# A convolutional row LSTM: the even pixels' gate product moved to GpSimd, the input gate taken in two parts, a new written order

## Chip, cores, metric

The kernel runs on one core of one Trainium2 chip. The metric is the device time of one execution in microseconds; the median of the runs is quoted.

## What is computed

The input x has 8 images of 96 channels, 128 rows and 128 pixels, in float32. It is normalised in 32 groups of channels over each image (group norm). A masked 1x3 convolution of every normalised row gives the input's share of four gates; its mask lets a pixel see its left neighbour and, by thirds of the channels, itself. Then an LSTM runs down the rows: the state h of a row is convolved along the row with three taps (left, same, right), and

```
gates = conv3(h) + bias + row of the input's convolution
f, i, o = sigmoid(three of them); g = tanh(the fourth)
c = f * c + i * g
h = o * tanh(c)
out[row] = x[row] + h
```

Each row needs the row before it, 128 times in turn.

## The kernel before

**Half steps.** The batch is cut in two halves of four images (s = 0 and 1). A half step n is row n // 2 of half n % 2. The halves take turns, so that one half's elementwise work can lie beside the other's matmuls: n depends on n - 2. There are 256 half steps, R = 4 rows make a block, and blocks are loaded and stored whole.

**Even and odd pixels.** Pixels of a row are split into even and odd ones (64 of each), so a half step's operand is 256 columns for each parity. The three-tap convolution is computed by a short algorithm: from the state come `vs` (even plus odd, method `total`, L571), `vf` (odd minus even, `difference`, L583), and `vd` (two shifted differences, `shifted`, L587). Four products of these with prepared weights, 1, 2, 0 and 3 (`H_PRODUCTS`, L365), and one sum and one difference in between give both parities. The same is done for the input's convolution: `own_image` (L322) makes three operands of one row set out of x, `widen` (normalise into a work buffer `xw`, L297), then a sum (L315) and a pair of differences (L316). These feed the products P, Q and E. The other 32 channels of x, which all gates share, are normalised into the state's tile by `normalise_shared` (L340).

**Gates in banks.** The 384 gate channels are three tiles A, B, C of 128 rows, each in a PSUM bank of 512 columns (even 256, odd 256). Rows 0 to 95 of A, B and C are the gates f, i and o; rows 96 to 127 of each are a third of g. A half step is 33 products: 1, 2, 0, 3 for three tiles, each in two halves of 64 weight rows, and P, Q, E for three tiles with 64 rows. Two row groups of 64 rows work side by side; `Lanes` (L372) deals the products out in turn, and lets a product wait for the other row group where both add to one bank.

**A half step's chain.** For each tile: products 1, 2 (and P, Q); `copy` (L508, ScalarE, adds the bias, PSUM to SBUF); `even` and `odd` (L512 and L516, VectorE, in PSUM); products 0, 3, E on top; then ScalarE's `tanh` (L520) and `sigmoid` (L527, in place in PSUM). Then `forget` f * c (L532, VectorE), `gated` i * g (L537, VectorE), `cell` (L547, VectorE), `cell_tanh` (L552, ScalarE), `output` (L560, VectorE), and the next operands vf, vs (VectorE) and vd (GpSimd). `residual` (L607, GpSimd) adds h to x. The tile framework lets a product on a bank wait for the last vector operation on that bank, whichever half it wrote.

**The written order.** The compiler's scheduler is off (`manual_schedule`); each engine runs its instructions in the order in which they are written. The string `PERIOD` (L678) writes one half step n. A name is a part (`PARTS`, L685) with its tile: `1A` is product 1 of tile A (its first half at the first naming, the second at the next), `cpA` copy, `loA` even, `hiA` odd, `ta` tanh, `si` sigmoid, `fg` forget, `gt` gated, `ce` cell, `th` cell_tanh, `ou` output, `S`, `F`, `D` the next total, difference and shifted, `re` residual. A mark ' means half step n - 1, '' n - 2, + n + 1. A last letter a or b after some parts (`SPLIT`, L684) takes even or odd pixels alone. `W` calls `prepare(n - 1)`, which emits the preparation of the next block that `work` (L640) assigns to that half step: `own_image` of one image of the half, then the shared norm of one image. So GpSimd's order in a period is vd, residual, widen, sum, differences, shared norm.

**Start.** Ahead of the loop the statistics of all images are gathered from chunks of 1 MB, and the first rows are written out by hand (events, L815). `FIRST` (L629) gives the preparation of the first half steps, in which more has to be done than later.

Of the kernel before, what the change touches and what calls it, by code (L numbers as in the profile page):

```python
# [8 lines left out]
AF = mybir.ActivationFunctionType  # L9
# [12 lines left out]
def kernel(  # L22
# [103 lines left out]
    xs = pair([P, R, 3, BH, J], "xs")  # L126
# [4 lines left out]
    xw = [const.tile([P, R, W + 1], F32, tag=f"xw{i}", name=f"xw{i}") for i in range(2)]  # L131
# [29 lines left out]
    E = mybir.EngineType  # L161
# [147 lines left out]
            s * BH + j,  # L309
        )  # L310

    def combine(xw, n, total, differences):

        e, o = xw[:, 0:n, 0:J], xw[:, 0:n, J + 1 :]
        nc.gpsimd.tensor_add(total, e, o)  # L315
        nc.gpsimd.tensor_sub(  # L316
            differences,
            strided(xw[:, 0, :], 0, [(W + 1, n), (J, 2), (1, J)]),
            strided(xw[:, 0, :], J + 1, [(W + 1, n), (0, 2), (1, J)]),
        )  # L320

    def own_image(s, k, j):  # L322

        to = xs[s][k % 2]
        widen(nc.gpsimd, xw[0], 0, R, s, k, j, 0)
        combine(xw[0], R, to[:, :, 0, j, :], to[:, :, 1:3, j, :])

    def own_row(xw, s, r, lo=0, hi=BH):

        to = xs[s][0]  # L330
        combine(
            xw[:, lo:hi],
            hi - lo,
            to[:, r, 0, lo:hi],
            to[:, r, 1:3, lo:hi].rearrange("p t b j -> p b t j"),
        )
# [19 lines left out]
    HB = BH * J  # L356
    NT = NB * R
    last = NT * NH - 1
# [49 lines left out]
    class HalfStep:  # L408


        def __init__(self, n):
            self.n, (self.row, self.s) = n, divmod(n, NH)
            self.ps, self.m1, self.moving, self.done, self.gates, self.th = {}, {}, {}, set(), None, None
            self.started, self.images, self.halves, self.writer = set(), {}, {}, {}
            self.hx = hx[self.s][self.row // R % 2][:, self.row % R]
            self.xs = xs[self.s][self.row // R % 2][:, self.row % R]
            self.c = cs[self.s].rearrange("p t b j -> p (t b j)")
# [34 lines left out]
        def own(self, a, i):  # L452

            low = a == order["A"] or (a == order["C"] and (self.s == 0 or (self.n, i) == (1, 2)))
            rhs = self.xs[:, i].rearrange("p b j -> p (b j)")
            self.mm(a, i % 2, wo[i], rhs, slice(0, C2) if low else slice(C2, P))
# [63 lines left out]
            nc.scalar.activation(self.part(g, lo, hi, t), self.part(ps, lo, hi, t), AF.Tanh)  # L520


        def sigmoid(self, a):
            if self.row == 0 and a == 0:
                return
            gate = self.ps[a][0:C]
            nc.scalar.activation(gate, gate, AF.Sigmoid)  # L527

        def forget(self):
            f = self.ps[0][0:C]  # L530
# [3 lines left out]
        def gated(self, lo=0, hi=BH, t=None):  # L534
            to = self.g if self.row > 0 else self.c
            to, i, g = (self.part(ap, lo, hi, t) for ap in (to, self.ps[1][0:C], self.g))
            nc.vector.tensor_mul(to, i, g)  # L537


        def part(self, ap, lo, hi, t=None):  # L540
            ap = ap.rearrange("p (t b j) -> p t b j", t=2, b=BH)
            return ap[:, :, lo:hi] if t is None else ap[:, t, lo:hi]
# [44 lines left out]
        def shifted(self, lo=0, hi=BH):  # L587
            h = self.hx[:, 0, lo, :]
            diff = nc.gpsimd.tensor_sub(  # L589
                self.operand("vd", 2)[:, :, lo:hi],  # L590
                strided(h, 1, [(BH * JP - 1, 2), (JP, hi - lo), (1, J)]),
                strided(h, 0, [(BH * JP + 1, 2), (JP, hi - lo), (1, J)]),
            )
            if self.last.ins.engine != E.Pool:
                tc.add_manual_dep(
                    diff.ins,
                    self.last.ins.name,
                    mybir.DependencyInfo(
                        mybir.DependencyClass.Sync, mybir.DependencyReason.SCHED_ONLY
                    ),  # L600
                    reason="GpSimd starts when VectorE is done with both SBUF reads",
                )

        def residual(self):
            s, row = self.s, self.row
            xo = xt[s, row // R][0:C, :, row % R, :].rearrange("p b (j t) -> p t b j", t=2)
            (nc.gpsimd if 2 * row + s < last else nc.vector).tensor_add(xo, xo, self.h)  # L607

    def store(s, k, lo, hi):
        nc.sync.dma_start(  # L610
# [7 lines left out]
    SHARED = (((0, 0, R), (3, 0, 1)), ((1, 0, R),), ((2, 0, R),), ((3, 1, R),))  # L618
# [10 lines left out]
    FIRST = [  # L629
        own(0, 0),  # L630
        own(0, 1),
        own(0, 2) + shared(0, 1, 0, 1),
        own(0, 3) + [(load_rows, 0, 2)] + shared(0, 1, 2, 3),
        own(1, 0, 1),
        own(1, 2) + shared(1, 1, 0, 1),
        own(1, 3) + [(load_rows, 1, 2)] + shared(1, 1, 2, 3),
        [(own_image, 0, 2, 0), (own_image, 1, 2, 0)],
    ]

    def work(n):  # L640
        if n < len(FIRST):
            return FIRST[n]
        row, s = divmod(n, NH)
        k, r = divmod(row, R)
        parts = []
        if r == R - 1 and k + 2 < NB:
            parts.append((own_image, s, k + 2, 0))
        elif r < R - 1 and k + 1 < NB:
            parts.append((own_image, s, k + 1, r + 1))
        if k + 1 < NB:  # L650
            parts += shared(s, k + 1, *SHARED[r])
        if r == R - 2 and k + 2 < NB:
            parts.append((load_rows, s, k + 2))
        return parts

    worked = set()

    def prepare(n):
        if n not in worked:
            worked.add(n)  # L660
            for part, *args in work(n):
                part(*args)

    def finish(n):
        prepare(n)
# [19 lines left out]
    PARTS = {  # L685
# [57 lines left out]
    late = []  # L743
# [106 lines left out]
    n = m = 0  # L850
    for b in range(B):
# [7 lines left out]
        for k in range(QW // CH):  # L859
# [11 lines left out]
            if alone:  # L871
                i = list(shares).index(k)
# [25 lines left out]
    j = BH - 1  # L898
# [104 lines left out]
```

## Time and profile before

| What | us |
|---|---|
| median of 3 runs | 2024.15 (2023.83 to 2025.46) |
| the profiled execution's own time | 2027.04 |
| its span, first to last instruction | 2025.2 |
| granted TensorE clock | 0.997 |
| L508 copy, ScalarE, 128x256, mean of one | 0.474 |
| L527 sigmoid, ScalarE, 96x512 | 0.577 |
| L520 tanh, ScalarE, 32x512; 32x256 | 0.592; 0.369 |
| L552 cell_tanh, ScalarE, 96x256 | 0.411 |
| L512, L516 even, odd, VectorE, 128x256 | 0.425, 0.422 |
| L532 forget, VectorE, 96x512 | 0.696 |
| L537 gated, L547 cell, L560 output, VectorE, 96x256 | 0.412, 0.410, 0.412 |
| L573 vs, L585 vf, VectorE, 128x256 | 0.427, 0.429 |
| L589 vd, L607 residual, GpSimd | 1.041, 1.297 |
| L297 widen, L315 sum, L316 differences, GpSimd | 0.816, 0.641, 1.070 |
| L297 shared norm, GpSimd, 32x512 | 0.816 |

How it is read: the page gives busy time by engine, the chain of work that ended last, and the costliest groups of instructions; the timeline gives instructions in order of time, with the idle time before each and what ended it in square brackets. Equal instructions in a row are merged (x2, with the time from the first start to the last end). An operation on an engine may start before the one ahead of it has ended: two 128x256 operations on VectorE follow each other at about 0.33 us. Times in the timeline count from the span's start. In the half steps of the loop, from some 210 us on, one period looks like the next.

### The profile page before, as it was taken

Reading aid. Unit: us, or ns where it says so; the run is one execution under the profiler, and the core shown is the slowest. Engines: PE = TensorE matmul, PEld = TensorE weight load, DVE = VectorE, ACT = ScalarE, POOL = GpSimd, SP = SyncE. Lnnn points to the kernel's source line nnn. Section 1 sums busy time; section 2 is a strip of 40 time slices with the busy share of each in tenths; the row PEclk is TensorE's granted clock in tenths of the full one; section 3 lists DMA queues with packets and bytes.
Section 4 is the critical chain, followed back from the end, with each engine's and each line's share of the span. In section 5 each row is a group of like instructions: output and inputs, shape, how many; then the busy total and the mean of one; then the engine's idle time right before and its main releaser. Section 6 shows DMA issues by size and latency. Waiting matters only on the chain.

```text
span 2025.2 us, 44842 instructions
## 1 busy us (share of the span) xinstructions
PE 1923.3 (95%) x16936; PEld 1831.0 (90%) x16936; DVE 1529.1 (76%) x3996; ACT 1494.9 (74%) x3161; POOL 1473.1 (73%) x1712
## 2 busy tenths in 40 slices
PE   0289999999999999999999999999999999999998
PEld 0178999999999999999999999999999999999997
DVE  5767777777777777777777777777777777777776
ACT  3776777777777777777777777777777777777776
POOL 3348777777777777777777777777777777777752
PEclk9989999999999999999999999999999999999999
DMA  9994333444334334433433443343344333434411
GB/s 374 424 310 100 98 103 91 112 115 104 82 89 113 92 101 115 113 83 82 110 95 95 116 116 95 79 100 96 93 116 116 96 82 96 107 92 106 116 33 32
DMA packets 103382, 237.11 MB, mean 117 GB/s; under 512 B 5952, under 2 KB 8896, under 8 KB 97280
## 3 DMA queue, kind: packets, MB, share of 16 engines
q1 hardware_dynamic: 103168, 234.25, 42.0%
q8 instruction: 135, 2.21, 0.5%
q14 instruction: 79, 0.65, 0.1%
HBM read 183.90 MB, written 50.33 MB: 116 GB/s over the span
## 4 chain that ended last, share of the span: by engine, by line
PE 93%; DMA 4%; ACT 2%; DVE 1%; issue 0%; SPq 0%; POOL 0%; DVEq 0%; POOLq 0%
PE ps L442 92%; DMA piece<-in_x_dram 3%; DMA xs<-in_x_dram 1%; ACT piece L216 1%; PE ps L174 0%; ACT piece L217 0%; DVE bst L876 0%; ACT hx L295 0%; ACT piece L295 0%; DVE hx L560 0%; ACT xs L216 0%; ACT xs L217 0%; SPq L864 0%; PE pv L251 0%; DVE ps L516 0%
## 5 line engine op out<-in xcount | busy, mean ns | idle before, releaser
L442 PE MATMUL ps<-vd,wl 64*128 64x256 f32 (+1 forms) x6096 | 1390.9, 379 | 0.3
L442 PEld LDWEIGHTS ps<-vd,wl 64*128 64x128 f32 (+1 forms) x6096 | 1028.4, 186 | 45.7 <-issue 2.4
L442 PE MATMUL ps<-vs,wm 64*128 64x256 f32 (+1 forms) x3052 | 775.1, 380 | 4.9 <-POOL vs L573 4.4
L442 PE MATMUL ps<-vf,wm 64*128 64x256 f32 (+1 forms) x3052 | 766.3, 377 | 0.0
L527 ACT ACTIVATE ps<-ps 96x512 f32<-96x512 f32 x766 | 441.6, 577 | 356.2 <-PE ps L442 348.1
L442 PE MATMUL ps<-xs,wx 64*128 64x256 f32 x3080 | 637.8, 377 | 11.1 <-POOL xs L315 11.1
L589 POOL TENSOR_TENSOR vd<-hx 128x512 f32<-128x512 f32 x257 | 266.7, 1038 | 388.5 <-PE ps L442 384.8
L442 PEld LDWEIGHTS ps<-xs,wx 64*128 64x128 f32 x3080 | 494.0, 187 | 14.2 <-POOL xs L315 11.6
L520 ACT ACTIVATE g<-ps 32x256 f32<-32x256 f32 (+1 forms) x1021 | 468.6, 482 | 26.7 <-PE ps L442 6.3
L442 PEld LDWEIGHTS ps<-vf,wm 64*128 64x128 f32 (+1 forms) x3052 | 475.4, 187 | 11.0 <-PE ps L442 0.4
L442 PEld LDWEIGHTS ps<-vs,wm 64*128 64x128 f32 (+1 forms) x3052 | 459.6, 186 | 21.6 <-POOL vs L573 5.4
L512 DVE TENSOR_TENSOR ps<-m,ps 128x256 f32<-128x256 f32 x768 | 326.0, 425 | 192.5 <-ACT m L508 182.0
L442 PE MATMUL ps<-xs,wt 64*128 64x256 f32 x1530 | 453.2, 377 | 0.6 <-DVE ps L516 0.6
L508 ACT ACTIVATE m<-ps,wl 128x256 f32<-128x256 f32 x766 | 361.6, 474 | 90.9 <-PE ps L442 84.3
L532 DVE TENSOR_TENSOR ps<-ps,c 96x512 f32<-96x512 f32 x254 | 176.8, 696 | 232.9 <-PE ps L442 226.9
L607 POOL TENSOR_TENSOR x<-x,hx 96x512 f32<-96x512 f32 x255 | 330.8, 1297 | 6.7 <-DVE hx L560 6.7
L516 DVE TENSOR_TENSOR ps<-m,ps 128x256 f32<-128x256 f32 x768 | 300.8, 422 | 1.3 <-PE ps L442 1.2
L442 PEld LDWEIGHTS ps<-xs,wt 64*128 64x128 f32 x1530 | 280.0, 186 | 12.8 <-DVE ps L516 1.0
L316 POOL TENSOR_TENSOR xs<-xw 128x512 f32<-128x512 f32 (+1 forms) x254 | 270.9, 1067 | 0.0
L297 POOL TENSOR_SCALAR hx<-x,rstd,nmr 32x384 f32<-32x384 f32 (+2 forms) x312 | 225.8, 724 | 33.2 <-DMA x<-in_x_dram 1.1
L297 POOL TENSOR_SCALAR xw<-xr,rstd,nmr 128x512 f32<-128x512 f32 x252 | 205.6, 816 | 7.1 <-DVE nmr L289 6.5
L537 DVE TENSOR_TENSOR g<-ps,g 96x256 f32<-96x256 f32 x507 | 189.0, 413 | 3.8 <-ACT g L520 3.8
(91 smaller groups left out, 1223.1 us busy)
## 6 DMA issues: line engine op xcount, KB each, us to landing
xr<-in_x_dram SPq DMA_DIRECT2D x124, 512.0 KB, 6.4
x<-in_x_dram SPq DMA_DIRECT2D x63, 768.0 KB, 6.1
out_dram<-x SPq DMA_DIRECT2D x62, 768.0 KB, 4.6
xs<-in_x_dram SPq DMA_DIRECT2D x30, 1024.0 KB, 12.3
piece<-in_x_dram SPq DMA_DIRECT2D x16, 1024.0 KB, 12.3
x<-in_x_dram SPq DMA_DIRECT2D x62, 256.0 KB, 3.2
xs<-in_x_dram SPq DMA_DIRECT2D x4, 512.0 KB, 8.7
out_dram<-x SPq DMA_DIRECT2D x2, 576.0 KB, 3.7
```

Source lines behind the costliest of these rows:

```text
L297: return engine.tensor_scalar(dst, src, scale, shift, ALU.mult, ALU.add)
L316: nc.gpsimd.tensor_sub(differences, strided(xw[:, 0, :], 0, [(W + 1, n), (J, 2), (1, J)]), strided(xw[:, 0, :], J + 1, [(W + 1, n), (0, 2) ...
L442: made = nc.tensor.matmul(self.ps[a][:, bass.ts(half, HB)][:, cols], weights[rows, bass.ts(a, P)], rhs[rows, cols], start=new, stop=False, ...
L508: nc.scalar.activation(self.m1[a], m1, AF.Identity, bias=column)
L512: nc.vector.tensor_add(self.ps[a][:, 0:HB], self.m1[a], self.ps[a][:, HB:])
L516: nc.vector.tensor_sub(hi, self.m1[a], hi)
L520: nc.scalar.activation(self.part(g, lo, hi, t), self.part(ps, lo, hi, t), AF.Tanh)
L527: nc.scalar.activation(gate, gate, AF.Sigmoid)
L532: nc.vector.tensor_mul(f, f, self.c)
L537: nc.vector.tensor_mul(to, i, g)
L589: diff = nc.gpsimd.tensor_sub(self.operand("vd", 2)[:, :, lo:hi], strided(h, 1, [(BH * JP - 1, 2), (JP, hi - lo), (1, J)]), strided(h, 0, ...
L607: (nc.gpsimd if 2 * row + s < last else nc.vector).tensor_add(xo, xo, self.h)
```

## The change

- `gated` for even pixels goes to GpSimd. It reads the even half of the input gate from a new SBUF tile `i`, and g; the odd pixels' product stays on VectorE and reads PSUM.
- `sigmoid` of tile B is split: `siBa` writes the even half to that SBUF tile, `siBb` the odd half in place.
- `prepare` has three parts, called at `U`, `V` and `W`. In the steady loop U is empty, V emits the shared norm, W `own_image` and the loads. On GpSimd a period's order in the built program becomes vd, residual, shared norm, even gate product, widen, sum, differences.
- `PERIOD` is written anew. TensorE's order is 2A 2B 1A 1B 0C' 1A 3C' 2A 2B 0C' 1B 3C' 2C EC' 1C PB+ PC+ 1C 0A 2C 3A QC+ EA 3B QA+ EB QB+ 0B PA+ 3A 0B 0A 3B; ScalarE's siBa' taB' siA' siBb' cpA cpB taA' taCb' taCa' siC' cpC thb' tha'; VectorE's hiC' fg' loA hiA loB gtb' hiB ceb' cea' loC oub' oua' F' S'.
- `residual` waits for the total of the half step after it in the same half, where that was on VectorE (`hold`).
- The first half steps' preparation is spread differently: five shared norms of the second block go to ScalarE, and two images of half 1 are prepared in pieces with the second work buffer (`apart`, `LATER`).

Line numbers grow by up to 36: vf is L602 after, vs L590, vd L606, the sum L314, the differences L318, the gate product L552 or L554.

```diff
+    def add_pixels(xw, n, total):
+
+        nc.gpsimd.tensor_add(total, xw[:, 0:n, 0:J], xw[:, 0:n, J + 1 :])
+
+    def subtract_pixels(xw, n, differences):
+
         nc.gpsimd.tensor_sub(
             differences,
...
+    def combine(xw, n, total, differences):
+
+        add_pixels(xw, n, total)
+        subtract_pixels(xw, n, differences)
...
-        def sigmoid(self, a):
+        def sigmoid(self, a, lo=0, hi=BH, t=None):
             if self.row == 0 and a == 0:
                 return
-            gate = self.ps[a][0:C]
-            nc.scalar.activation(gate, gate, AF.Sigmoid)
+            gate = self.part(self.ps[a][0:C], lo, hi, t)
+            if t == 0:
+                self.even_input = self.tile("i", (C, HB))
+                to = self.even_input.rearrange("p (b j) -> p b j", b=BH)
+            else:
+                to = gate
+            nc.scalar.activation(to, gate, AF.Sigmoid)
...
-            nc.vector.tensor_mul(to, i, g)
+            if t == 0 and self.even_input is not None:
+                i = self.even_input.rearrange("p (b j) -> p b j", b=BH)
+                nc.gpsimd.tensor_mul(to, i, g)
+            else:
+                nc.vector.tensor_mul(to, i, g)
...
-            if self.last.ins.engine != E.Pool:
+            self.hold(diff)
+
+        def hold(self, made):
+            if self.last is not None and self.last.ins.engine != E.Pool:
                 tc.add_manual_dep(
-                    diff.ins,
+                    made.ins,
                     self.last.ins.name,
...
-            (nc.gpsimd if 2 * row + s < last else nc.vector).tensor_add(xo, xo, self.h)
+            made = (nc.gpsimd if 2 * row + s < last else nc.vector).tensor_add(xo, xo, self.h)
+            following = steps.get(self.n + NH)
+            if self.n < last and following is not None:
+                following.hold(made)
...
+    def on_scalar(s, k, *images):
+        return [(normalise_shared, nc.scalar, s, k, j, 0, R) for j in images]
+
+    def apart(s, k, j):
+        to = xs[s][k % 2]
+        return (
+            (widen, nc.gpsimd, xw[1], 0, R, s, k, j, 0),
+            (add_pixels, xw[1], R, to[:, :, 0, j, :]),
+            (subtract_pixels, xw[1], R, to[:, :, 1:3, j, :]),
+        )
+
+    spread = apart(1, 1, 0)
     FIRST = [
...
+        (on_scalar(0, 1, 0), [spread[0]], own(0, 3) + [(load_rows, 0, 2)]),
+        (on_scalar(0, 1, 1), list(spread[1:]), own(1, 1)),
+        (on_scalar(0, 1, 2) + on_scalar(1, 1, 2), shared(0, 1, 3), own(1, 2)),
+        (on_scalar(1, 1, 3), shared(1, 1, 0, 1), own(1, 3) + [(load_rows, 1, 2)]),
+        ([], [], [(own_image, 0, 2, 0)]),
     ]
+    LATER = dict(zip((11, 13, 15), apart(1, 2, 0)))
...
-        parts = []
-        if r == R - 1 and k + 2 < NB:
-            parts.append((own_image, s, k + 2, 0))
-        elif r < R - 1 and k + 1 < NB:
-            parts.append((own_image, s, k + 1, r + 1))
-        if k + 1 < NB:
-            parts += shared(s, k + 1, *SHARED[r])
+        early, late = shared(s, k + 1, *SHARED[r]) if k + 1 < NB else [], []
+        if n in LATER:
+            early.append(LATER[n])
+        ahead, image = (k + 2, 0) if r == R - 1 else (k + 1, r + 1)
+        if ahead < NB:
+            late.append((own_image, s, ahead, image))
         if r == R - 2 and k + 2 < NB:
-            parts.append((load_rows, s, k + 2))
-        return parts
+            late.append((load_rows, s, k + 2))
+        return [], early, late
...
-        "2A hiC' siA' D'' 1B 1A taA' 2B fg' 3C' 1A 0C' re'' taB' 2A 2B EC' 1B cpA 0C' 2C W loA cpB "
-        "3C' 1C siB' loB PB+ QA+ hiA taCb' 2C hiB taCa' 0A gtb' 1C siC' gta' EA 0B ceb' cpC 3A PA+ "
-        "cea' thb' PC+ 3B loC tha' QC+ oub' EB oua' QB+ 3A F' 3B 0A S' 0B"
+        "2A hiC' 2B 1A U siBa' 1B 0C' taB' D'' 1A 3C' siA' 2A 2B siBb' 0C' fg' 1B cpA re'' 3C' 2C "
+        "cpB V loA EC' 1C taA' PB+ hiA PC+ taCb' loB 1C 0A taCa' gtb' 2C 3A gta' W siC' hiB QC+ "
+        "EA ceb' cpC 3B cea' QA+ thb' loC EB tha' QB+ oub' 0B PA+ oua' 3A F' 0B 0A S' 3B"
...
-    SPLIT = ("taC", "gt", "ce", "th", "ou")
+    SPLIT = ("taC", "siB", "gt", "ce", "th", "ou")
...
-            if name == "W":
-                prepare(n - 1)
+            if name in "UVW":
+                prepare(n - 1, range("UVW".index(name) + 1))
                 continue
```

More of the change, by code (lines that the diff above doesn't have):

```diff
@@ L310, in widen @@
         )
-    def combine(xw, n, total, differences):
-        e, o = xw[:, 0:n, 0:J], xw[:, 0:n, J + 1 :]
-        nc.gpsimd.tensor_add(total, e, o)
+    def add_pixels(xw, n, total):
+        nc.gpsimd.tensor_add(total, xw[:, 0:n, 0:J], xw[:, 0:n, J + 1 :])
+    def subtract_pixels(xw, n, differences):
         nc.gpsimd.tensor_sub(
@@ L414, in __init__ @@
             self.started, self.images, self.halves, self.writer = set(), {}, {}, {}
+            self.even_input = self.last = None
             self.hx = hx[self.s][self.row // R % 2][:, self.row % R]
@@ L627, in shared @@
         ]
-    FIRST = [
[L630 to L637, printed above, removed]
+    def on_scalar(s, k, *images):
[8 more added lines that the diff above has]
+    spread = apart(1, 1, 0)
+    FIRST = [
+        ([], [], own(0, 0)),
+        ([], [], own(0, 1)),
+        ([], [], own(0, 2)),
+        (on_scalar(0, 1, 0), [spread[0]], own(0, 3) + [(load_rows, 0, 2)]),
[3 more added lines that the diff above has]
+        ([], [], [(own_image, 0, 2, 0)]),
     ]
+    LATER = dict(zip((11, 13, 15), apart(1, 2, 0)))
     def work(n):
@@ L644, in work, with prepare @@
         k, r = divmod(row, R)
-        parts = []
-        if r == R - 1 and k + 2 < NB:
-            parts.append((own_image, s, k + 2, 0))
-        elif r < R - 1 and k + 1 < NB:
-            parts.append((own_image, s, k + 1, r + 1))
-        if k + 1 < NB:
-            parts += shared(s, k + 1, *SHARED[r])
+        early, late = shared(s, k + 1, *SHARED[r]) if k + 1 < NB else [], []
[4 more added lines that the diff above has]
+            late.append((own_image, s, ahead, image))
         if r == R - 2 and k + 2 < NB:
-            parts.append((load_rows, s, k + 2))
-        return parts
+            late.append((load_rows, s, k + 2))
+        return [], early, late
     worked = set()
[L658 to L662, printed above, removed]
+    def prepare(n, parts=(0, 1, 2)):
+        for i in parts:
+            if (n, i) not in worked:
+                worked.add((n, i))
+                for part, *args in work(n)[i]:
+                    part(*args)
     def finish(n):
```

## Prediction

> **What bounds the kernel now.** I read the busy shares and the chain that ended last, then the timeline of one period in the middle of the run, engine by engine. The page says where to look:
>
> ```profile
> PE 1923.3 (95%) x16936; PEld 1831.0 (90%) x16936; DVE 1529.1 (76%) x3996; ACT 1494.9 (74%) x3161; POOL 1473.1 (73%) x1712
> PE 93%; DMA 4%; ACT 2%; DVE 1%; issue 0%; SPq 0%; POOL 0%; DVEq 0%; POOLq 0%
> ```
>
> TensorE ends nearly everything. But a full row is not a full engine, so count. A half step has 33 products; each is two passes on one of two row groups, and in the timeline a row group starts a pass every 0.216 us (1004.55 and 1004.77). 33 x 2 x 0.216 / 2 = 7.12 us. The period is 7.33 (GpSimd's shifted difference, L589, starts at 1001.90 and 1009.23 below). So 0.21 us a period is stall, and it sits in one place:
>
> ```profile
> 1004.80 0.38 PE L442 MATMUL ps<-vs,wm 64*128 64x256 f32 x1
> 1004.99 0.63 PE L442 MATMUL ps<-xs,wx 64*128 64x256 f32 x4
> 1005.42 0.59 PE L442 MATMUL ps<-vf,wm 64*128 64x256 f32 x2
> 1005.77 0.45 PE L442 MATMUL ps<-vd,wl 64*128 64x256 f32 x1
> ```
>
> The vd product is 0A, due on its row group at 1004.80 + 3 x 0.216 = 1005.45; it starts at 1005.77, 0.15 after hiA, the first of the two L516 below, has ended (1005.20 + 0.42). The row group loses two slots, 0.43 us; the groups change places every period, so each loses that in every second one. That is all TensorE can give back: 0.21 x 250 periods, some 54 us. The other engines of that period:
>
> ```profile
> 1003.89 0.94 ACT L508 ACTIVATE m<-ps,wl 128x256 f32<-128x256 f32 x2 [0.31 <-PE ps L442]
> 1005.33 0.65 ACT L520 ACTIVATE g<-ps 32x256 f32<-32x256 f32 x2
> ```
> ```profile
> 1005.20 0.76 DVE L516 TENSOR_TENSOR ps<-m,ps 128x256 f32<-128x256 f32 x2
> 1006.53 0.74 DVE L547 TENSOR_TENSOR c<-ps,g 96x256 f32<-96x256 f32 x2
> 1008.30 0.42 DVE L585 TENSOR_TENSOR vf<-hx 128x256 f32<-128x256 f32 x1
> 1008.64 0.42 DVE L573 TENSOR_TENSOR vs<-hx 128x256 f32<-128x256 f32 x1
> ```
> ```profile
> 1001.90 1.04 POOL L589 TENSOR_TENSOR vd<-hx 128x512 f32<-128x512 f32 x1 [1.55 <-PE ps L442]
> 1004.18 0.81 POOL L297 TENSOR_SCALAR xw<-xr,rstd,nmr 128x512 f32<-128x512 f32 x1
> 1005.67 1.07 POOL L316 TENSOR_TENSOR xs<-xw 128x512 f32<-128x512 f32 x1
> 1006.85 0.82 POOL L297 TENSOR_SCALAR hx<-x,rstd,nmr 32x512 f32<-32x512 f32 x1
> 1009.23 1.04 POOL L589 TENSOR_TENSOR vd<-hx 128x512 f32<-128x512 f32 x1 [1.57 <-PE ps L442]
> ```
>
> See here that GpSimd is done at 1007.67 and idles 1.57 us, just while VectorE makes vf and vs (1008.30 to 1009.06), the only two VectorE operations of the period with both inputs in SBUF. Early in the run, where there is more to prepare, that is not so:
>
> ```profile
> 200.66 0.42 DVE L585 TENSOR_TENSOR vf<-hx 128x256 f32<-128x256 f32 x1
> 201.00 1.29 DVE L573 TENSOR_TENSOR vs<-hx 128x256 f32<-128x256 f32 x1
> ```
> ```profile
> 200.70 1.31 POOL L316 TENSOR_TENSOR xs<-xw 128x512 f32<-128x512 f32 x1
> ```
>
> vf goes through, L316 is stretched from 1.07 to 1.31, and vs takes 1.29 instead of 0.42: it ends 0.28 after L316. The next forget product (L532) follows the last by 8.11 us (202.69 to 210.80) instead of 7.33. One such meeting costs 0.78 us.
>
> **What the Trainium skill says.** "SBUF — State Buffer", section "SBUF: two separate sides": VectorE (with two SBUF inputs) and GpSimd share a port pair, "an exclusive lock, not a bandwidth split", and who starts first keeps it for the whole instruction. The rows above agree, 1.29 beside 0.42; with one exception: at 169.69 a vf that began 0.09 us after a GpSimd operation still took only 0.44. "GPSIMD Engine Reference", section "4.1 Engine selection": GpSimd has no PSUM port, and two-input elementwise work is about twice as slow there. That is why the even input gate must go to SBUF; the second half agrees (0.64 us for L315's 128x256 beside 0.41 for a gated product), no run shows the first.
>
> **The change, part by part.**
>
> *hiA ahead of loB.* Two 0.33 steps of VectorE's queue become one: hiA starts when loA has ended, 0.34 us earlier against TensorE. The wait of 0.32 at 0A goes. Next late is hiB, now behind the odd gated product: the 11th product of a period begins 2.16 after the first, is readable 0.63 later (as in before: 1003.73, cpB at 1004.36), then cpB 0.37, taA 0.62 to the start of taCb, 0.41 to gtb, 0.33 to hiB, 0.42 long, 0.15 to the product 3B, which has five slots of 0.43 to the next period: 7.25. So with nothing else TensorE would gain 0.09 of the 0.21.
>
> *The input gate in two parts.* ScalarE: one 0.58 us operation becomes two of 0.37 to 0.47 (rows of 256 columns from PSUM; I take 0.4), +0.2 us. It had 1.38 + 0.31 us of idle time, and both parts are done before cpB's data arrive; nothing. Without that cover, 0.2 a period.
>
> *The even gated product on GpSimd.* VectorE sheds 0.33, off its path. The product starts 0.08 after taCa ends (one ScalarE-to-GpSimd handover at 140.95 to 141.03) and takes 0.64, the L315 row; bounds 0.6 and 0.7. It ends 0.72 after taCa, and the even cell sum would start at 0.76 in VectorE's own queue: no loss. Behind it waits the rest of GpSimd's queue.
>
> *own_image after it.* This is the step that decides. In the built program GpSimd's order is vd, residual, shared norm, gated product, widen, sum, differences, vd. Before, the three of own_image began at 1004.18, tied to nothing. Now they hang on taCa. From its end: product 0.08 to 0.72; widen at once; differences (L318 after) 1.48 later, the distance in before (1004.18 to 1005.67): start 2.20, 1.07 long. VectorE from the same end: loC waits for cpC (siC 0.63, cpC 0.47) at 1.14, the output products 0.33 and 0.33 later, vf 0.44 after the second: 2.24. **Both start within 0.05 us, every period**, and only a shift of over 0.3 would part them. By the exception above (0.09 and still through) vf wins: it ends at 2.67, the differences 0.93 later as at 200.7 (3.60), vs 0.28 after that (3.88), where it would have ended at 3.00. Behind vs in VectorE's queue stand hiC and forget; behind its product in TensorE's queue (the third of the period) stands everything; GpSimd's vd waits for it too, with 2 us to spare.
>
> The cycle from vs to vs: 0.09 to the third product (0A's load began 0.05 after its releaser's semaphore, the pass 0.03 later), 4 x 0.43 to the 11th, 0.63 to cpB, 0.37 + 0.62 + 0.29 + 0.36 to the end of taCa, 3.88 to the end of vs: 7.97. Against 7.33 it is +0.635; the single meeting of before, 0.78, is near it.
>
> *Other order, holds, spread.* vf is now wanted by the first two products and vs by the third, which spares vs 0.2 us, already in the count. The residual's new hold is on a vs that vd has waited for already; nothing. Banks are taken in the order B, C, A, of products long read; nothing. load_rows stays behind the same readers on SP and lands (6.4 us) a block ahead; nothing. Five 32x512 norms move to ScalarE at 0.84 (L295): 0 to 4 us, I take 1.
>
> *Sum.* own_image is in some 238 steady periods: 238 x 0.635 = 151. The first seven periods last 59.1 us already (153.75 to 212.8), 8.4 each, and 7 x 7.97 = 55.8: -3, with the norms -2. The last eight, without own_image: 8 x -0.09 = -1, and I round the small terms to -1 in all, since the first periods may keep part of their length. The profiled execution took 2027.0 (span 2025.2): 2177. The median of the runs shown is 2.9 below it: **2174**.
>
> **The rivals.** *A: the differences get the port first.* For: by the row they start 0.05 sooner, and the page says the first keeps it. Then vf ends 0.28 after them: 0.08 + 0.64 + 1.48 + 1.07 + 0.28 = 3.55 after taCa; vf to vf 0.09 + 2.16 + 0.63 + 1.64 + 3.55 = 8.07, +0.735 x 238 - 1: 2198. *B: they don't meet, and it is faster.* If GpSimd reaches the differences over 0.3 us later than I count, vf and vs are both ahead and GpSimd waits instead, with time to spare. Then hiB's 7.25 holds, -0.09 x 245 = -22: 2002. For it: my handovers have few samples. Against: 0.3 is half of the gated product. *C: partly.* The chain is shorter than counted or meets only in some periods: 2060 to 2140. *D: no change*, if hiB's wait is longer and they don't meet.
>
> **How the numbers follow.** vs waits: 0.52, 2174 (2160 to 2190). A: 0.24. C: 0.07. B: 0.14. D: 0.03. A measurement here can tell about 0.2%, 4 us. Faster 0.14, same 0.03, slower 0.83. B and D are left out of the range; with half of C it is 2100 to 2212.
>
> **What would show it.** Right: vs (L590 after) near 1.3 us, the differences near 1.3, a period of 7.9 to 8.1, GpSimd's idle time before the gated product and not before vd, TensorE below 90% and waiting for vs. A: vf long instead (over 1 us). Wrong: vf and vs at 0.42 each, a period under 7.33, or the differences clear of both.

## The result and the profile after

The changed kernel took 2241.32 us (median of 4 runs, 2239.16 to 2242.4) beside 2024.17 of the kernel before: a ratio of 1.107, 95% interval [1.1051, 1.1089], 217 us slower. The profiled execution took 2242.4 with a span of 2240.3, at a granted clock of 0.997 as before. The forecast was 2174, in a range of 2100 to 2212. So the sign was right and the size was 67 us short.

The busy shares and the chain that ended last, of the page after:

```profile
PE 2077.2 (93%) x16936; PEld 1851.2 (83%) x16936; DVE 1702.8 (76%) x3743; ACT 1537.4 (69%) x3419; POOL 1709.5 (76%) x1960
...
DVE 43%; PE 29%; ACT 14%; DMA 8%; POOL 3%; issue 2%; SPq 0%; POOLq 0%; DVEq 0%
```

TensorE made 93% of the chain before. Now the chain runs through all three engines of a half step, as it does when each period waits for the one before it. VectorE has 253 instructions fewer and 173.7 us more of busy time (1529.1 before). The costliest groups of the page show where that is:

```profile
L552 POOL TENSOR_TENSOR g<-i,g 96x256 f32<-96x256 f32 x253 | 183.2, 724 | 235.1 <-ACT g L528 233.3
...
L318 POOL TENSOR_TENSOR xs<-xw 128x512 f32<-128x512 f32 (+1 forms) x254 | 326.8, 1287 | 0.1
...
L590 DVE TENSOR_TENSOR vs<-hx 128x256 f32<-128x256 f32 (+1 forms) x254 | 289.8, 1141 | 0.0
```

The mean of a vs is 1141 ns, and it was 426 before; the differences take 1287 instead of 1067. The timeline shows two periods in the middle of the run, VectorE (two stretches) and then GpSimd:

```profile
1001.50 0.42 DVE L602 TENSOR_TENSOR vf<-hx 128x256 f32<-128x256 f32 x1
1001.85 1.29 DVE L590 TENSOR_TENSOR vs<-hx 128x256 f32<-128x256 f32 x1
...
1009.77 0.43 DVE L602 TENSOR_TENSOR vf<-hx 128x256 f32<-128x256 f32 x1
1010.11 1.29 DVE L590 TENSOR_TENSOR vs<-hx 128x256 f32<-128x256 f32 x1
```
```profile
1001.51 1.34 POOL L318 TENSOR_TENSOR xs<-xw 128x512 f32<-128x512 f32 x1
...
1007.56 0.72 POOL L552 TENSOR_TENSOR g<-i,g 96x256 f32<-96x256 f32 x1
...
1009.77 1.34 POOL L318 TENSOR_TENSOR xs<-xw 128x512 f32<-128x512 f32 x1
```

vf and the differences start within 0.01 us of each other, vf goes through, and vs then stands until some 0.28 us after the differences have ended (1001.51 + 1.34 = 1002.85; vs ends at 1003.14). The gate product (L552) ends at 1008.28, and the differences follow it by 1.49: this is what ties them to vf. It is the meeting that the forecast described. What the page does not show is the period itself. I took it from the trace, from one forget product (L545, L532 before) to the next: 7.334 us before and 8.197 after (medians of the 17th to 240th period; here "the middle", 224 periods), where the forecast had 7.97. The middle holds 198.7 of the difference (1643.3 us before, 1842.0 after), the start and the first 16 periods 11.8, the last 13 periods 4.6.

### The profile page after: what moved, and what is told of

Same layout as the page of the kernel before. It is cut to its first block, busy times and chain, and to the rows that moved or that the text cites. A ratio compares the mean times of both kernels' runs of the same rounds, so it can differ in the third digit from the quotient of the medians.

```text
span 2240.3 us, 45488 instructions
## 1 busy us (share of the span) xinstructions
PE 2077.2 (93%) x16936; PEld 1851.2 (83%) x16936; DVE 1702.8 (76%) x3743; ACT 1537.4 (69%) x3419; POOL 1709.5 (76%) x1960
## 4 chain that ended last, share of the span: by engine, by line
DVE 43%; PE 29%; ACT 14%; DMA 8%; POOL 3%; issue 2%; SPq 0%; POOLq 0%; DVEq 0%
PE ps L450 28%; DVE vs L590 11%; ACT g L528 10%; DVE c L564 7%; DVE hx L577 7%; DVE vf L602 6%; ACT m L516 5%; DVE g L554 4%; DVE ps L520 3%; DMA xs<-in_x_dram 3%; DVE ps L524 3%; DMA out_dram<-x 3%; DMA x<-in_x_dram 2%; DVE bst L912 1%; POOL x L627 1%
## 5 line engine op out<-in xcount | busy, mean ns | idle before, releaser
L450 PEld LDWEIGHTS ps<-vd,wl 64*128 64x128 f32 (+1 forms) x6096 | 975.2, 186 | 91.4 <-DVE ps L524 45.1
L450 PE MATMUL ps<-vs,wm 64*128 64x256 f32 (+1 forms) x3052 | 806.6, 400 | 52.9 <-DVE vs L590 48.5
L450 PE MATMUL ps<-xs,wx 64*128 64x256 f32 x3080 | 722.4, 383 | 11.1 <-POOL xs L314 11.1
L450 PE MATMUL ps<-vf,wm 64*128 64x256 f32 (+1 forms) x3052 | 708.6, 382 | 13.0 <-DVE vf L602 12.9
L450 PEld LDWEIGHTS ps<-vs,wm 64*128 64x128 f32 (+1 forms) x3052 | 422.5, 185 | 157.1 <-DVE vs L590 133.6
L516 ACT ACTIVATE m<-ps,wl 128x256 f32<-128x256 f32 x766 | 361.5, 473 | 187.0 <-PE ps L450 163.9
L528 ACT ACTIVATE g<-ps 32x256 f32<-32x256 f32 (+1 forms) x1021 | 467.9, 481 | 21.6 <-PE ps L450 6.2
L540 ACT ACTIVATE i<-ps 96x256 f32<-96x256 f32 x253 | 96.1, 380 | 423.1 <-PE ps L450 380.5
L540 ACT ACTIVATE ps<-ps 96x512 f32<-96x512 f32 x766 | 363.5, 501 | 14.2
L606 POOL TENSOR_TENSOR vd<-hx 128x512 f32<-128x512 f32 x257 | 266.3, 1036 | 131.4 <-DVE vs L590 130.6
L552 POOL TENSOR_TENSOR g<-i,g 96x256 f32<-96x256 f32 x253 | 183.2, 724 | 235.1 <-ACT g L528 233.3
L524 DVE TENSOR_TENSOR ps<-m,ps 128x256 f32<-128x256 f32 x768 | 322.3, 420 | 10.0 <-PE ps L450 1.2
L545 DVE TENSOR_TENSOR ps<-ps,c 96x512 f32<-96x512 f32 x254 | 176.7, 696 | 197.7 <-ACT ps L540 197.7
L318 POOL TENSOR_TENSOR xs<-xw 128x512 f32<-128x512 f32 (+1 forms) x254 | 326.8, 1287 | 0.1
L590 DVE TENSOR_TENSOR vs<-hx 128x256 f32<-128x256 f32 (+1 forms) x254 | 289.8, 1141 | 0.0
```

What stands on the lines that cost most here:

```text
L318: nc.gpsimd.tensor_sub(differences, strided(xw[:, 0, :], 0, [(W + 1, n), (J, 2), (1, J)]), strided(xw[:, 0, :], J + 1, [(W + 1, n), (0, 2) ...
L450: made = nc.tensor.matmul(self.ps[a][:, bass.ts(half, HB)][:, cols], weights[rows, bass.ts(a, P)], rhs[rows, cols], start=new, stop=False, ...
L516: nc.scalar.activation(self.m1[a], m1, AF.Identity, bias=column)
L524: nc.vector.tensor_sub(hi, self.m1[a], hi)
L540: nc.scalar.activation(to, gate, AF.Sigmoid)
L545: nc.vector.tensor_mul(f, f, self.c)
```

## The experiments

All times below are medians of 4 runs with the kernel before beside them on the same chip (2023.7 to 2024.3). Periods are medians of the middle; a time given as "after vs" counts from the start of vs, unless its end is named.

**e1: the even gate product back on VectorE.** The new order stays, and the product again reads PSUM.

```diff
-            if t == 0:
-                self.even_input = self.tile("i", (C, HB))
-                to = self.even_input.rearrange("p (b j) -> p b j", b=BH)
-            else:
-                to = gate
-            nc.scalar.activation(to, gate, AF.Sigmoid)
+            nc.scalar.activation(gate, gate, AF.Sigmoid)
```

> The changed kernel with the even gate product back on VectorE, which reads the input gate in PSUM as before; the gate is still taken in two parts, both in place, and the new order stays. Port theory (the whole loss is the meeting of own_image's differences on GpSimd with vf and vs on VectorE): GpSimd no longer waits for the gate product, own_image runs right behind the shared norm and is through before vf; vs and vf take 0.42, the period is 7.25 to 7.45, the time 2005 to 2050. Order theory (the new written order makes the chain long, and the long vs is only where it shows): the period stays above 8.0, the time above 2190. Gate theory (the slower product on GpSimd itself is the loss): 0.3 a period less, 2160 to 2180.

Measured: 2138.04, ratio 1.0564 [1.0548, 1.0579]; period 7.716; vs takes 0.42, and the differences are over at 6.4 us after vs, a microsecond before vf. The meeting is gone from all but 28 of the 224 periods, and a loss of 0.38 a period remains that none of the three theories had: the new order itself costs something. In the 28, vf or vs is still held; they are the only long periods, and they cost 16 us of the 114. In each of the 28 the shared norm, which e1 leaves ahead of `own_image`, waits for its load first, and `own_image` runs late.

**e2: no differences.** From the third block on the differences of the next block's image are not computed, so that a part of the input's convolution is left out.

```diff
-        combine(xw[0], R, to[:, :, 0, j, :], to[:, :, 1:3, j, :])
+        add_pixels(xw[0], R, to[:, :, 0, j, :])
+        if k < 2:
+            subtract_pixels(xw[0], R, to[:, :, 1:3, j, :])
```

> The changed kernel without own_image's differences from the third block on (left out: the operands of products Q and E keep old values, so part of the input's convolution isn't computed). The gate product stays on GpSimd, and behind it stand only widen and sum. Port theory: vf and vs at 0.42, a period of 7.4 as in the last periods of the changed kernel, where no own_image is left; time 2040 to 2065. Order or gate theory: above 2200.

**e3: the differences deferred.** All the work is done, but GpSimd computes the differences after the next half step's vd (a new name X in the written order, behind D'').

```diff
-        "2A hiC' 2B 1A U siBa' 1B 0C' taB' D'' 1A 3C' siA' ...
+        "2A hiC' 2B 1A U siBa' 1B 0C' taB' D'' X 1A 3C' siA' ...
```

> The changed kernel with own_image's differences moved to stand behind the next period's vd on GpSimd; all work is done, and the gate product stays on GpSimd. Port theory: L318's new place is clear of vf and vs, the differences take 1.07, the period is 7.4 to 7.5, the time 2035 to 2070; the gate product may start some 0.1 later in periods with two norms. Order or gate theory: above 2200.

Measured: e2 2081.43, ratio 1.0287 [1.0271, 1.0302]; e3 2116.96, ratio 1.0454 [1.0437, 1.0472]. Both have the same period, 7.42. So the meeting is worth 8.197 - 7.424 = 0.773 a period, whether the differences are taken away or moved. Both times lie above the ranges of the port theory, 16 and 47 us: without the meeting the kernel is still slower than before, in two ways: 7.42 is 0.09 above the 7.334 of before, and some periods are far longer (over 8 us in 25 of 224 in e2 and 49 in e3, up to 9.2 and 10.8; the middle's sum less 224 medians is 32.7 us in e2 and 64.4 in e3, and 5.9 in the changed kernel). One such period of e3, VectorE and then GpSimd:

```profile
527.91 0.42 DVE L570 TENSOR_TENSOR c<-ps,g 96x256 f32<-96x256 f32 x1 [1.59 <-POOL g L558]
...
529.35 0.42 DVE L608 TENSOR_TENSOR vf<-hx 128x256 f32<-128x256 f32 x1
529.70 0.42 DVE L596 TENSOR_TENSOR vs<-hx 128x256 f32<-128x256 f32 x1
```
```profile
525.72 1.35 POOL L297 TENSOR_SCALAR hx<-x,rstd,nmr 32x512 f32<-32x512 f32 x2 [1.16 <-DMA x<-in_x_dram]
527.15 0.72 POOL L558 TENSOR_TENSOR g<-i,g 96x256 f32<-96x256 f32 x1
...
531.26 1.07 POOL L318 TENSOR_TENSOR xs<-xw 128x512 f32<-128x512 f32 x1
```

vf and vs take 0.42 and the differences (L318) come behind them in 1.07: the meeting is gone. The even cell sum (L570) waits 1.59 us for the gate product (L558), which stands behind two shared norms (merged in one row), which wait for the block's load. In the kernel before nothing that VectorE needs stands behind these norms.

**b3: the meeting alone, in the kernel before.** Its own written order and its gate products on VectorE; only `own_image` is put behind the even gate product by an added dependency, as in the changed kernel, so that the differences fall on vf.

```diff
+        made = widen(nc.gpsimd, xw[0], 0, R, s, k, j, 0)
+        if k > 1:
+            tc.add_manual_dep(made.ins, product[0].ins.name, ...)
...
-        "... 0C' 2C W loA cpB ... gta' EA 0B ceb' ...
+        "... 0C' 2C loA cpB ... gta' W EA 0B ceb' ...
```

> The kernel before, with one thing added: GpSimd's own_image waits for the even gate product on VectorE (no gate product on GpSimd, old order otherwise), so that its differences come to lie where vf and vs are. Port theory: vf or vs grows to 1.2 or 1.3, the period to 7.9 to 8.1, the time to 2165 to 2215. Order or gate theory: GpSimd has time to spare, the time stays within 2020 to 2040.

Measured: 2218.21, ratio 1.0957 [1.094, 1.0973]; period 8.153, both somewhat above what the port theory gave. VectorE and GpSimd of one period:

```profile
1005.12 1.26 DVE L596 TENSOR_TENSOR vf<-hx 128x256 f32<-128x256 f32 x1
1006.31 0.41 DVE L584 TENSOR_TENSOR vs<-hx 128x256 f32<-128x256 f32 x1
```
```profile
1005.04 1.06 POOL L316 TENSOR_TENSOR xs<-xw 128x512 f32<-128x512 f32 x1
```

Here the differences are 0.08 ahead, vf is held, and the period grows by 0.82. One meeting per period is enough for 194 of the changed kernel's 217 us.

**e4: e3 with the norms last.** GpSimd's shared norms come behind the next block's sum.

```diff
-        "... cpB V loA EC' 1C taA' ... gtb' 2C 3A gta' W siC' hiB QC+ "
+        "... cpB loA EC' 1C taA' ... gtb' 2C 3A gta' W V siC' hiB QC+ "
```

> The changed kernel with the differences put behind the next half step's vd (as in e3), and with GpSimd's shared norms moved from ahead of the even gate product to behind the next block's sum. All the work is done. e3 took 2117 us: a steady period of 7.42 us, and periods of 8 to 9.2 us two or three times in each eight half steps, 64 us in all over the 224 half steps in the middle of the run. Theory 1 (the gate product is queued behind two norms of 0.81 us, or behind one that waits for the x block's load): the long periods go, the steady one stays, 2117 - 64 x 253/224 = 2045, range 2035 to 2060. Theory 2 (the long periods come from the loads themselves, or from the deferred differences, wherever the norms stand): 2100 or more.

Measured: 2064.57, ratio 1.0197 [1.0182, 1.0212]. The long periods are gone (3.6 us above the median in the middle, no period over 7.51), and the middle takes 1666.6, which is e3's 1727.4 less its 64.4 and 4 more. That confirms the first theory. The total is 20 us above the number given and 5 above its range. In part the norms are now late in the first blocks: the first 16 periods take 139.2 instead of e3's 132.4, one of them 14.7. In part the number may have been too low: of the 72 us that it took off, 64 are in the middle, and the rest was an extension to all 253 periods.

**e5: another ScalarE order, in the changed kernel.** siBb and taA change places; the meeting stays.

```diff
-        "... siA' 2A 2B siBb' 0C' fg' 1B cpA re'' 3C' 2C "
-        "cpB V loA EC' 1C taA' PB+ ...
+        "... siA' 2A 2B taA' 0C' fg' 1B cpA re'' 3C' 2C "
+        "cpB V loA EC' 1C siBb' PB+ ...
```

> The changed kernel with two of ScalarE's operations in each other's place: the odd input gate (siBb, 0.36 us) behind cpB, and taA (0.59 us) ahead of cpA. The meeting of the differences with vs and vf stays. Theory 1 (cpB, taA, taCb, taCa follow each other on ScalarE without a gap, and this queue is on the path that sets the period): 0.23 us a period go over about 240 periods, 55 us, 2186; between 2175 and 2200. Theory 2 (taA waits for TensorE, not for its place in ScalarE's queue, or another engine is as late): 2230 to 2245.

Measured: 2177.08, ratio 1.076 [1.0742, 1.0778], and vs still takes 1.29. The period falls to 7.848, by 0.35. Over the middle that would be 78 us, but 24 periods are now over 8 us (17 us above the median in all): between 300 and 1950 us the even cell sum waits 20 times for the gate product, 13.6 us in all. ScalarE from cpB to taCa, of the changed kernel and of e5 (L516 is cpA and cpB, L528 tanh, L540 sigmoid):

```profile
1005.11 1.01 ACT L516 ACTIVATE m<-ps,wl 128x256 f32<-128x256 f32 x2 [0.62 <-PE ps L450]
1006.15 1.26 ACT L528 ACTIVATE g<-ps 32x512 f32<-32x512 f32 x3
```
```profile
1006.31 1.02 ACT L516 ACTIVATE m<-ps,wl 128x256 f32<-128x256 f32 x2
1007.23 0.37 ACT L540 ACTIVATE ps<-ps 96x256 f32<-96x256 f32 x1
1007.62 0.65 ACT L528 ACTIVATE g<-ps 32x256 f32<-32x256 f32 x2
```

From the start of the copies to the end of taCa it is 2.30 us in the changed kernel (1005.11 to 1007.41) and 1.96 in e5 (1006.31 to 1008.27). The sigmoid is not only shorter: it starts 0.10 before cpB has ended, and taA starts 0.03 after (medians: 0.372 from the start of cpB to that of siBb in e5, 0.498 to that of taA in the changed kernel).

**b1: hiA ahead of loB in the kernel before.** The new order has hiA there, and the forecast credited it with a period of 7.25.

```diff
-        "3C' 1C siB' loB PB+ QA+ hiA taCb' 2C hiB taCa' ...
+        "3C' 1C siB' hiA loB PB+ QA+ taCb' 2C hiB taCa' ...
```

> The kernel before with one operation moved: hiA ahead of loB on VectorE, so that TensorE's next group on bank A, which waits for hiA in the steady state, is released 0.33 us earlier. If this wait sets the period of 7.33 us, the period falls to between 7.12 (33 weight loads and products by two row groups) and 7.25 (ScalarE's and VectorE's chain from cpA on, with the wait gone): 1985 to 2005. If the chain from cpA (ScalarE, then VectorE, to vs) sets it, nothing changes or loB is late for bank B in its place: 2020 to 2045.

Measured: 2035.82, ratio 1.0056 [1.0041, 1.0071]; period 7.384, up 0.05. VectorE of one period in the kernel before, and of one in b1 (L512 is lo, L516 hi, L537 the gate products):

```profile
1004.39 0.90 DVE L512 TENSOR_TENSOR ps<-m,ps 128x256 f32<-128x256 f32 x2 [0.70 <-ACT m L508]
1005.20 0.76 DVE L516 TENSOR_TENSOR ps<-m,ps 128x256 f32<-128x256 f32 x2
1005.86 0.74 DVE L537 TENSOR_TENSOR g<-ps,g 96x256 f32<-96x256 f32 x2
```
```profile
1007.11 0.43 DVE L512 TENSOR_TENSOR ps<-m,ps 128x256 f32<-128x256 f32 x1 [0.79 <-ACT m L508]
1007.58 0.43 DVE L516 TENSOR_TENSOR ps<-m,ps 128x256 f32<-128x256 f32 x1
1007.91 0.42 DVE L512 TENSOR_TENSOR ps<-m,ps 128x256 f32<-128x256 f32 x1
1008.37 0.43 DVE L516 TENSOR_TENSOR ps<-m,ps 128x256 f32<-128x256 f32 x1
1008.71 0.74 DVE L537 TENSOR_TENSOR g<-ps,g 96x256 f32<-96x256 f32 x2
```

Between the starts of loA, hiA, loB and hiB lie 0.46, 0.34 and 0.46 in b1; between those of loA, loB, hiA and hiB before it was 0.47, 0.34 and 0.33. From loA to the first gate product it is therefore 1.60 instead of 1.47. Of these 0.13 only 0.05 reach the period, because loA starts 0.08 earlier after the end of vs. TensorE no longer waits for hiA there, but now it waits for vs. The vs of one period and the first product on it, before and in b1:

```profile
1001.31 0.42 DVE L573 TENSOR_TENSOR vs<-hx 128x256 f32<-128x256 f32 x1
1001.96 0.63 PE L442 MATMUL ps<-vs,wm 64*128 64x256 f32 x4
```
```profile
1004.10 0.42 DVE L573 TENSOR_TENSOR vs<-hx 128x256 f32<-128x256 f32 x1
1004.58 0.79 PE L442 MATMUL ps<-vs,wm 64*128 64x256 f32 x4
```

Before, the product starts 0.24 after vs has ended, and in step: 0.216 after the pass ahead of it on its row group (1001.75). In b1 it starts 0.05 after the end of vs, in every period. So b1 does two things at once: it frees TensorE of one wait, and it makes VectorE's queue longer. It shows that the freed wait does not make the kernel faster, since the round through vs is then the bound. What the wait alone was worth, with VectorE's queue as long as before, it does not show.

**c1: b1 with loC behind vs.** Bank C's products come later on TensorE to match.

```diff
-        "2A hiC' siA' D'' 1B 1A taA' 2B fg' 3C' 1A 0C' re'' taB' 2A 2B EC' 1B cpA 0C' 2C W loA cpB "
+        "2A loC' hiC' siA' D'' 1B 1A taA' 2B fg' 1A 2A 3C' re'' taB' 2B 0C' 1B cpA EC' 3C' 2C 0C' W loA cpB "
```

> As b1, and loC moved behind vs, to the start of the next half step, with bank C's products later on TensorE. VectorE's chain from hiB over the cell and the output to vf and vs loses 0.33 us. If VectorE's chain is what holds the period once hiA is first, the period comes to 7.12 to 7.2: 1970 to 1995. If TensorE's products on bank C, now 0.4 us later, are what cpA or siA waits for, it is no better than b1: 2000 to 2060.

Measured: 2347.46, ratio 1.1595 [1.1578, 1.1612], far above both expectations; periods of 8.18 and 9.10 take turns. siA starts 1.03 us after vs in every second period (0.65 in the others) and not at 0.30 as in b1, waiting for TensorE, and taA, taB and forget are late behind it. Which of the moved products holds it was not pursued.

**e7: e1 with hiB ahead of the gate products.** The old order has it there.

```diff
-        "... taCb' loB 1C 0A taCa' gtb' 2C 3A gta' W siC' hiB QC+ "
+        "... taCb' loB hiB 1C 0A taCa' gtb' 2C 3A gta' W siC' QC+ "
```

> e1 (the changed kernel with the even gate product back on VectorE) with one operation moved: hiB from behind the two gate products to ahead of them, where the old written order has it. e1 has a period of 7.716 us and no meeting. Theory 1 (what e1 loses against the kernel before is hiB's place: with both products on VectorE it stands on the path between taCb and vs): gtb starts 0.06 us later, ceb 0.27 earlier, period 7.44, 2138 - 0.27 x 250 = 2070, range 2060 to 2085. Theory 2 (the new order of TensorE's products or of ScalarE's activations is what e1 loses by): 2115 or more.

Measured: 2069.11, ratio 1.022 [1.0205, 1.0235]; period 7.389. So 0.33 of the 0.38 that e1 lost was hiB's place. The new order puts hiB where VectorE waits for GpSimd's product; with both products on VectorE there is no such hole. The 45 us that are left are not 0.055 a period alone: as in e1, vf or vs is held in some periods (44 of the 224 are long for it), and this costs 25 us.

**e8: e4 with the old written order.** The product on GpSimd, without a meeting and with nothing ahead of it.

```diff
-        "2A hiC' 2B 1A U siBa' 1B 0C' taB' D'' X 1A 3C' ...
+        "2A hiC' U siA' D'' X 1B 1A taA' 2B fg' 3C' 1A 0C' re'' taB' 2A 2B EC' 1B cpA 0C' 2C loA cpB "
+        "3C' 1C siBa' siBb' loB PB+ QA+ hiA taCb' 2C hiB taCa' 0A gtb' 1C siC' gta' W V EA 0B ceb' cpC 3A PA+ "
+        "cea' thb' PC+ 3B loC tha' QC+ oub' EB oua' QB+ 3A F' 3B 0A S' 0B"
```

> e4 (gate product on GpSimd, image behind it, differences behind the next vd, norms last) with the old written order in place of the new one, the input gate's two parts side by side at the old place behind cpB. There is no meeting and nothing ahead of the gate product. Theory 1 (the product on GpSimd ends at about 5.56 us after vs, VectorE's at 5.30 in the kernel before, and cea, which the kernel before starts at 5.55, waits for it: VectorE is given 0.33 us of time but cannot start the cell earlier): period 7.33 to 7.40, and with the 20 us that e4's start costs 2035 to 2060, no faster than the kernel before. Theory 2 (VectorE's queue from loB to vs is the path and the product's 0.33 us comes off it): period 7.0 to 7.12, 1985 or less.

Measured: 2067.2, ratio 1.0215 [1.0198, 1.0232]; period 7.459, somewhat above the first theory's 7.40, and the time 7 us above its range (the two sigmoids side by side take 0.78 where one took 0.61). The second theory's 7.0 to 7.12 is far off. VectorE of e8:

```profile
1005.82 0.42 DVE L570 TENSOR_TENSOR c<-ps,g 96x256 f32<-96x256 f32 x1
1006.46 0.42 DVE L570 TENSOR_TENSOR c<-ps,g 96x256 f32<-96x256 f32 x1 [0.22 <-POOL g L558]
```

The even cell sum waits 0.22 us for GpSimd. The product on GpSimd ends 5.63 after vs where VectorE's ended at 5.30, and the kernel before starts the even cell at 5.55. So the 0.33 us taken off VectorE is given back ahead of the even cell sum. No version that I ran beats the kernel before.

## Why the prediction was right or wrong, step by step

**Right: the meeting, and which way it goes.** "Both start within 0.05 us, every period": over the 224 periods of the middle the differences start between 0.008 us ahead of vf and 0.037 behind it. vf goes through in 198 and vs takes 1.29 (forecast 1.29); in 26 the differences are first and vf takes 1.34, which was rival A. The two take turns in one run, and the step from one to the other lies at a distance of zero, to about 5 ns. So the Trainium skill's sentence ("SBUF — State Buffer", section "SBUF: two separate sides") that the first to start keeps the port holds for these two operations as closely as that. That vf won in most periods was luck. My sums had the differences 0.04 ahead, and the exception that I built on, a vf that got through 0.09 after a GpSimd operation, was with a norm (L297), not with a difference. b3's vf, 0.06 to 0.10 after the differences, was held in all 224 periods. In the trace vf is first, by 0.01 us in the median. A period that goes over to a held vf is 0.10 longer, one that comes back from it 0.05.

**Wrong: the size of the period, 7.97 forecast and 8.20 measured.** The forecast's chain, from the end of vs to the end of the next:

| step | forecast | measured |
|---|---|---|
| end of vs to start of cpB | 0.09 + 1.72 + 0.63 = 2.44 | 2.515 |
| cpB to taA | 0.37 | 0.498 |
| taA, taCb, taCa | 0.62 + 0.29 + 0.36 | 0.615 + 0.285 + 0.361 |
| end of taCa to end of vs | 3.88 | 3.922 |
| sum | 7.96 | 8.196 |

Measured are medians over the middle. (The prediction wrote its sum as 7.97.) Three terms make the 0.24. *cpB to taA* is 0.13 of it: I took the distance from cpB to a sigmoid of the kernel before and used it for a tanh; e5, which puts a sigmoid there, shows the 0.372. *End of vs to cpB* is 0.075: bank C's product 0C' needs hiC, and the prediction itself put hiC behind vs in VectorE's queue, but counted its four slots as free. The page after charges weight loads of vd products with 45.1 us of waiting for L524, the line of all hi operations (1.0 for the same operations in the trace before). That this is hiC and that it is the 0.075 is my reading of the timeline (hiC ends at 1003.48, the product starts at 1003.73); no run took them apart. *End of taCa to vs* is 0.04: the gate product takes 0.724 (forecast 0.64, bounds 0.6 and 0.7, so outside them) and the later steps are a little shorter. Where 224 times the forecast's 0.635 make 142, the middle is 198.7 us longer: there lie 56 of the missing 67 us.

**Wrong: what the new order gives without a meeting.** The forecast was 7.25, and rival B rested on it. e4 has 7.424. The step that failed is the path from hiB to the next cpB, and two terms on it. *The path.* The forecast went from hiB to TensorE's product 3B and through TensorE to cpB. In e4 it goes from 3B to siBa and through ScalarE's queue, which is full:

```profile
1002.30 0.38 ACT L546 ACTIVATE i<-ps 96x256 f32<-96x256 f32 x1 [1.64 <-PE ps L456]
1002.69 0.59 ACT L534 ACTIVATE g<-ps 32x512 f32<-32x512 f32 x1
1003.31 0.85 ACT L546 ACTIVATE ps<-ps 96x512 f32<-96x512 f32 x2
1004.18 0.90 ACT L522 ACTIVATE m<-ps,wl 128x256 f32<-128x256 f32 x2
1005.10 1.26 ACT L534 ACTIVATE g<-ps 32x512 f32<-32x512 f32 x3
```

From siBa to taCa there is not one gap. The round that closes in e4, each step a median of the middle: hiB to 3B 0.054 from end to start, 3B to siBa 2.841, siBa to cpB 2.254, cpB to the odd gate product 1.518, from there to hiB 0.341, hiB 0.416 long. That is 7.424, the whole period.

Against the forecast, 3B to cpB is 5.10 instead of 4.94 (five slots, 2.16 and 0.63), and cpB to the odd gate product 1.52 instead of 1.40; hiB to 3B is 0.10 shorter. In the second is the same term as above, 0.37 for cpB to taA, which is 0.49 in e4. In the first, ScalarE's queue holds *the input gate in two parts*, which was priced at "nothing": siBa takes 0.39 of the queue and siBb 0.38. The prediction named the cover (ScalarE's idle 0.31 ahead of cpA), but not that the new order moves both parts ahead of cpA and so uses it up: siBb ends 0.03 before cpA starts. That the second part is what makes this path the longer one is not shown; no run has one part in the new order. With the meeting cpA waits for TensorE again (0.63 us), and the parts cost nothing.

*hiA ahead of loB* was counted as two steps of 0.33 that become one. In b1 hiA follows loA at 0.46, and VectorE's queue grows by 0.13. In the changed kernel and in e4 this is covered, since the odd gate product waits for ScalarE (0.33 and 0.16 us).

**Right and wrong: the even product on GpSimd.** "No loss" holds for the cell, but only because the new order fills the hole with hiB (e7 and e8). That it brings no gain even alone was not said. The shared norm ahead of it, with its wait for a load, was overlooked; in the changed kernel the meeting leaves room for it (of the 5.9 us above the median 3.8 are periods that go over to a held vf or come back from one); without the meeting it costs up to 64 (e3). "GPSIMD Engine Reference", section "4.1 Engine selection", on the half speed of two-input work is borne out: 0.724 beside VectorE's 0.41 for the same 96x256.

**Wrong: a sign to look for.** TensorE was to fall below 90% busy; it shows 93%, and 97% between 700 and 1700 us. The trace gives a pass 0.38 us although a row group starts one every 0.216, so that the passes of two row groups overlap in this row and hide short waits. The weight loads show it: 83% of the span, 90% before.

**The start.** I put the small terms at -1; the start and the first 16 periods cost 11.8 in all. It is mostly the same meeting: vf or vs is held in all of these 16 periods, in 6 of them before.

## What to carry to other kernels

When work is put behind another engine's result, ask at what moment of that engine's queue it will now run: two operations tied to the same release meet in every period and not now and then. To move an operation to a slower engine gains only what its consumer can use; compare the end of the operation there with the start of the consumer now, not the time taken off the faster engine. And the one wait that a busy engine shows is not what its removal gives: find the round that closes next and is nearly as long, and see that the edit does not make that one longer.

## What the runs showed of the hardware

A norm on GpSimd (`tensor_scalar`, one tensor input) does not hold VectorE back as a difference of two tensors does, when it starts inside a vf. In e4 it starts 0.14 to 0.19 us after vf in all 224 periods of the middle; vs, next in VectorE's queue, still takes 0.42, and the 32x512 norm takes 1.21 instead of 0.81. VectorE and GpSimd of e4:

```profile
1008.73 0.42 DVE L608 TENSOR_TENSOR vf<-hx 128x256 f32<-128x256 f32 x1
1009.08 0.42 DVE L596 TENSOR_TENSOR vs<-hx 128x256 f32<-128x256 f32 x1
```
```profile
1008.90 1.20 POOL L297 TENSOR_SCALAR hx<-x,rstd,nmr 32x512 f32<-32x512 f32 x1
```

Differences at that distance do hold vs: in e1 and e7 nine start 0.09 to 0.21 us after vf, and vs takes 1.28 or 1.29 each time. So the distance does not decide. The kind of operation may; another difference is that a sum stands right ahead of these differences, without a gap, and 0.10 ahead of the norm. No run took the two apart.

A norm that starts just ahead of vf lets it through, too: by 0.09 (before), 0.06 (e7) and 0.005 (c1), with a vf of 0.43 to 0.44. By the starts that the trace gives, these three do not follow the sentence on the first to start. Four norms of the kernel before that start 0.26 to 0.54 ahead and end inside vf hold it: it takes 0.47 to 0.64 and ends 0.27 to 0.28 after the norm. Where between 0.09 and 0.26 this turns was not tried.

A held VectorE operation ends 0.28 us after the difference that held it: 0.278 to 0.287 in all 448 periods of the middle of the changed kernel and b3.
